# The output stage of a two-layer block in a written order of steps, with the group norm inside the gate's weights

## The chip, the cores and the metric

The kernel runs on one core of a Trainium2 chip. The metric is the time of one execution on the device in microseconds; the figure used is the median of several runs. A core has five engines that run side by side, each with its own queue of instructions worked off in order: TensorE (PE in the profile, its weight loads PEld), VectorE (DVE), ScalarE (ACT), GpSimd (POOL) and SyncE (SP), which here only issues DMAs. Engines wait for each other through semaphores.

## The reference

All data are float32. The input is a 256 x 256 image with 128 channels, that is 65,536 positions. Layer 0 is a triangle-like attention over group-normalized and layer-normalized pairs; layer 1 is a selective-scan block (four scan directions, 256 inner channels, 16 states). Both add to their input. The change concerns the end of layer 1, which is, per position:

```python
xz = gn(x1) @ w_in.T                 # group norm of layer 0's output x1, 32 groups over the whole image
xi, z = split(xz, 2)                 # 256 channels each
z = silu(z)                          # the gate
...                                  # xi goes through a convolution and four scans and becomes y
mu = y.mean(-1); var = ((y - mu) ** 2).mean(-1)
y = (y - mu) / sqrt(var + 1e-5) * ln_w + ln_b    # layer norm over 256 channels
out = x1 + (y * z) @ w_out.T         # 256 channels to 128
```

The group norm subtracts a mean and multiplies by an inverse deviation, one of each per channel once the statistics of the whole image are known (`gn2`, a tile of 128 x 2).

## The kernel before

The kernel goes through the image in stages, each of which keeps its result in device memory: group statistics, pair norm, attention, convolution, a transposition of scan inputs, the scans, and last `output`. The scans take nearly all of the time. They leave `mid_y`, the sum of the four directions, as 65,536 rows of 256 channels. `mid_x1T` is x1 with channels on the partitions (128 x 65,536).

`output` (L917 to L979) runs over 64 blocks of TB = 1024 positions, each with two chunks of T = 512. The loops are unrolled in the program, so every block has instructions of its own. The function is written block by block, one step after another; in which order the instructions of different blocks stand in each engine's queue is decided by a planner, which interleaves them by estimated costs. (In the scans the order is written out by hand, under `tc.manual_schedule()`; `output` has none.)

For one block:

- SyncE loads `xt` (0.5 MB, L938) and `y` (1 MB, eight tiles of 128 rows, L940). Both come from a pool with three buffers for each.
- VectorE makes `xn`, the group-normalized `xt` (L942), in one operation of 128 x 1024.
- For each of the eight row tiles of `y`, VectorE makes statistics (L946, L947). ScalarE takes the square root of the eight variances (Sqrt, L949), VectorE the reciprocal (L951), and then normalizes the eight row tiles in place (L953).
- For each chunk and each half h of the 256 channels: TensorE multiplies `wz` with `xn` into `pz` (L961), ScalarE makes Silu of it (L962). TensorE transposes four row tiles of `y` into `pt` (L965), ScalarE applies layer-norm scale and bias on the way out of PSUM into `yz` (Identity, L966).
- GpSimd multiplies `yz` by `z`, both halves in one operation (L969).
- TensorE multiplies with `wo`, the two halves added up in `pw` (L972). VectorE adds `xt` (`r`, L974), TensorE transposes it back (`pr`, L977), ScalarE copies it to `ot` (L978). After the second chunk ScalarE's queue issues the store to `out` (L979).

PSUM has two buffers each for `pz` and `pt`, one each for `pw` and `pr`. All SBUF tiles but the loads (`yz`, `z`, `r`, `ot`, `mv` and so on) have two buffers. Silu and Sqrt need different tables in ScalarE, and a table load is placed ahead of the first operation that needs the other one.

The start of `output` waits for the end of the scans: its buffers take the place of theirs, and `y` is read from what the last store of the scans wrote (L821).

Of the kernel before, what the change touches and what calls it, by code (L numbers as in the profile page):

```python
# [28 lines left out]
F32 = mybir.dt.float32  # L29
AF = mybir.ActivationFunctionType  # L30
ALU = mybir.AluOpType
AX = mybir.AxisListType
PSUM = bass.MemoryType.PSUM
ds = bass.ds

P = 128
N = 256
NT = N * N
C = 128
H, HD = 4, 32  # L40
DI = 256
NH = DI // P
# [4 lines left out]
T = 512  # L47
# [149 lines left out]
def attention(tc, io, c):  # L197


    nc = tc.nc  # L200
    NJ = N // P
    GB = 4
    RB = BLK // N
    with tc.tile_pool(name="c_w", bufs=1) as wp, tc.tile_pool(name="c_io", bufs=2) as iop, tc.tile_pool(
# [7 lines left out]
        for name in ("Wq", "Wk", "Wv", "Wg", "Wo"):  # L212
            w[name] = wp.tile([P, P], F32, name=name)
            nc.sync.dma_start(out=w[name], in_=io[name])
        bias = wp.tile([P, NJ, H, N], F32, name="bias")
        for jt in range(NJ):
            for h in range(H):
                nc.sync.dma_start(
                    out=bias[:, jt, h, :],
                    in_=io["bias"][h].rearrange("(t j k) -> t j k", t=NJ, k=N)[jt],  # L220
                )

        with tc.For_i(0, NB // GB, 1, name="rows") as it:
# [36 lines left out]
            def scores(g, s, r):  # L260
                qs, kt, _ = qkvs[g, s]
                sc = [ap.tile([P, H, N], F32, name="sc") for _ in range(NJ)]
                nm = [ap.tile([P, H], F32, name="nm") for _ in range(NJ)]
                for hh in range(H // 2):
# [650 lines left out]


def output(tc, io, c):  # L917
    nc = tc.nc
    out = io["out"].rearrange("b h w c -> (b h w) c")
    TB = 1024  # L920
    NJ = TB // P
    QJ = T // P
    with tc.tile_pool(name="f_w", bufs=1) as wp, tc.tile_pool(name="f_in", bufs=3) as inp, tc.tile_pool(
        name="f_sb", bufs=2
    ) as sb, tc.tile_pool(name="f_ps", bufs=2, space=PSUM) as psum, tc.tile_pool(
        name="f_po", bufs=1, space=PSUM
    ) as po:
        wz = wp.tile([P, DI], F32, name="wz")
        nc.sync.dma_start(out=wz, in_=io["w_inT"][:, DI : 2 * DI])
        wo = wp.tile([P, NH, C], F32, name="wo")  # L930
        nc.sync.dma_start(out=wo, in_=io["w_outT"].rearrange("(h p) c -> p h c", p=P))
        ln = wp.tile([P, 2, NH], F32, name="ln")
        nc.sync.dma_start(out=ln[:, 0, :], in_=io["ln_w"].rearrange("(h p) -> p h", p=P))
        nc.sync.dma_start(out=ln[:, 1, :], in_=io["ln_b"].rearrange("(h p) -> p h", p=P))
        for b in range(NT // TB):
            cols = slice(b * TB, (b + 1) * TB)
            xt = inp.tile([P, TB], F32, name="xt")
            nc.sync.dma_start(out=xt, in_=io["x1T"][:, cols])  # L938
            y = inp.tile([P, NJ, DI], F32, name="y")
            nc.sync.dma_start(out=y, in_=io["y"][cols, :].rearrange("(j p) c -> p j c", p=P))  # L940
            xn = sb.tile([P, TB], F32, name="xn")
            nc.vector.tensor_scalar(xn, xt, c.gn2[:, 0:1], c.gn2[:, 1:2], ALU.subtract, ALU.mult)  # L942
            st = sb.tile([P, NJ, 6], F32, name="st")
            mv = sb.tile([P, NJ, 2], F32, name="mv")
            for j in range(NJ):
                nc.vector.bn_stats(st[:, j, :], y[:, j, :])  # L946
                nc.vector.bn_aggr(mv[:, j, :], st[:, j, :])  # L947
            sd = sb.tile([P, NJ], F32, name="sd")
            nc.scalar.activation(sd, mv[:, :, 1], AF.Sqrt, bias=c.eps)  # L949
            rs = sb.tile([P, NJ], F32, name="rs")  # L950
            nc.vector.reciprocal(rs, sd)  # L951
            for j in range(NJ):
                nc.vector.tensor_scalar(y[:, j, :], y[:, j, :], mv[:, j, 0:1], rs[:, j : j + 1], ALU.subtract, ALU.mult)  # L953
            ot = sb.tile([P, NJ, C], F32, name="ot")
            for s in range(TB // T):
                cs = slice(s * T, (s + 1) * T)
                yz = sb.tile([P, NH, T], F32, name="yz")
                z = sb.tile([P, NH, T], F32, name="z")
                for h in range(NH):
                    pz = psum.tile([P, T], F32, name="pz")  # L960
                    nc.tensor.matmul(pz, wz[:, h * P : (h + 1) * P], xn[:, cs], start=True, stop=True)  # L961
                    nc.scalar.activation(z[:, h, :], pz, AF.Silu)  # L962
                    pt = psum.tile([P, QJ, P], F32, name="pt")
                    for j in range(QJ):
                        nc.tensor.transpose(pt[:, j, :], y[:, s * QJ + j, h * P : (h + 1) * P], c.ident)  # L965
                    nc.scalar.activation(  # L966
                        yz[:, h, :], pt.rearrange("p j t -> p (j t)"), AF.Identity, bias=ln[:, 1, h : h + 1], scale=ln[:, 0, h : h + 1]
                    )
                nc.gpsimd.tensor_tensor(yz, yz, z, ALU.mult)  # L969
                pw = po.tile([P, T], F32, name="pw")  # L970
                for h in range(NH):
                    nc.tensor.matmul(pw, wo[:, h, :], yz[:, h, :], start=(h == 0), stop=(h == NH - 1))  # L972
                r = sb.tile([P, T], F32, name="r")
                nc.vector.tensor_tensor(r, pw, xt[:, cs], ALU.add)  # L974
                pr = po.tile([P, QJ, C], F32, name="pr")
                for j in range(QJ):
                    nc.tensor.transpose(pr[:, j, :], r[:, j * P : (j + 1) * P], c.ident)  # L977
                nc.scalar.copy(ot[:, s * QJ : (s + 1) * QJ, :], pr)  # L978
            nc.scalar.dma_start(out=out[cols, :].rearrange("(j p) c -> p j c", p=P), in_=ot)  # L979


SCRATCH = {
# [14 lines left out]
@with_exitstack  # L997
def build(ctx: ExitStack, tc: tile.TileContext, io):
    const = ctx.enter_context(tc.tile_pool(name="const", bufs=1))
    c = load_consts(tc, const, io)  # L1000
    group_stats(tc, io, c)
    pair_norm(tc, io, c)
    attention(tc, io, c)
    conv(tc, io, c)
    swap(tc, io, "dc1", "dcT")
    scans(tc, io, c)
    output(tc, io, c)
# [45 lines left out]
```

## Time and profile before

| what | us |
|---|---|
| median of 3 runs | 29,773.57 |
| lowest and highest run | 29,766.73 and 29,790.43 |
| profiled execution | 29,807.18 |
| its span on the core | 29,805.5 |
| last store of the scans issued (L821) | 29,023.53 |
| first load of `output` issued (L929) | 29,027.80 |
| first and last `pw` product begin (L972) | 29,048.7 and 29,796.2 |

The span is the time from the first to the last instruction on the core. Times within it count from its start. Over the 760 us from 29,040 to 29,800 the engines are busy as follows:

| engine | busy us | share |
|---|---|---|
| TensorE | 649.8 | 85% |
| ScalarE | 569.8 | 75% |
| VectorE | 555.5 | 73% |
| GpSimd | 305.7 | 40% |
| DMA engines (mean of 16) | | 54%, 172 GB/s |

The granted clock of TensorE is 1.00 of full speed in this stretch (0.955 over the whole span). Matrix instructions are pipelined: one begins before the one ahead of it has ended, so their durations add up to more than the time they take. A line of the groups gives line, engine, operation, tiles written and read, shapes and count, then busy time and the mean of one, then the idle time of the engine just before them, and which instructions ended it. A line of the chain gives the start, the length and the instructions. A float32 product of 512 columns is two matrix instructions in the profile.

### The profile page before, as it was taken

The page shows a single profiled execution, that of the slowest core. Times are in us where ns is not written, and L with a number is a line of the kernel's source. Part 1 is how long each engine was busy: PE and PEld are TensorE (multiplying, and loading weights), DVE is VectorE, ACT ScalarE, POOL GpSimd, SP SyncE. Part 2 cuts the span into 40 slices and gives each one's busy share as a digit, 9 for nine tenths or more (in the row PEclk, how much of TensorE's full clock was granted, in tenths as well). Part 3 has the DMA queues.
Part 4 walks back from the last instruction along what each step waited for, and adds up shares of the span by engine and source line. Part 5 has one row for each costly group of instructions (what it writes and reads, how often), then busy time and mean ns, then how long its engine had stood idle before and what let it go on. Part 6 is the DMA issues. An engine that isn't in the chain of part 4 may idle for free. (4 is left out here: it accounts for less than half of the span.)

```text
span 29805.5 us, 535143 instructions
## 1 busy us (share of the span) xinstructions
PE 27420.7 (92%) x196490; PEld 22683.4 (76%) x196490; DVE 25716.6 (86%) x28349; ACT 25280.5 (85%) x49640; POOL 23015.2 (77%) x10118
## 2 busy tenths in 40 slices
PE   8888899699999999999999999999999999999998
PEld 3444444488888888888888888888888888888884
DVE  4555566599999999999999999999999999999997
ACT  5555422499999999999999999999999999999997
POOL 1333200299999999999999999999999999999984
PEclk8888899899999999999999999999999999999999
DMA  5000144433333333333333333333333333333335
GB/s 194 35 36 35 52 116 113 114 130 130 130 130 127 130 127 129 131 130 127 131 127 130 129 129 130 130 129 131 127 130 128 131 130 128 129 130 129 129 129 172
DMA packets 1924053, 3630.55 MB, mean 122 GB/s; under 512 B 532298, under 2 KB 1240010, under 8 KB 1889491
## 3 DMA queue, kind: packets, MB, share of 16 engines
q1 hardware_dynamic: 1424722, 3339.77, 32.9%
q10 hardware_dynamic: 496640, 255.88, 3.1%
q8 instruction: 1571, 25.74, 0.4%
q14 instruction: 1120, 9.17, 0.1%
HBM read 3002.42 MB, written 592.84 MB: 121 GB/s over the span
## 5 line engine op out<-in xcount | busy, mean ns | idle before, releaser
L784 POOL TENSOR_TENSOR hs<-hs,cc 128x1024 f32<-128x1024 f32 x8192 | 19303.7, 2374 | 1672.5 <-DVE state L783 1163.9
L781 DVE TENSOR_TENSOR_SCAN hs<-da,state,mm 128x1024 f32<-128x1024 f32 x8192 | 19227.4, 2347 | 1023.5 <-PE mm L771 694.9
L769 PE MATMUL mm<-dg,dxt 128*128 128x128 f32 x65536 | 9421.6, 288 | 1255.7 <-DVE hs L781 1019.1
L769 PEld LDWEIGHTS mm<-dg,dxt 128*128 128x128 f32 x65536 | 8249.9, 197 | 2747.3 <-DVE hs L781 2080.7
L762 ACT ACTIVATE da<-delta,A 128x1024 f32<-128x1024 f32 x8192 | 9342.2, 1140 | 91.2 <-PEq L903 59.8
L540 PE MATMUL y<-ident,hs 128*128 128x128 f32 x65536 | 8464.1, 274 | 0.0
L758 ACT ACTIVATE but<-dxt,bt 128x256 f32<-128x256 f32 x16384 | 8172.8, 499 | 11.4 <-DVE dxt L717 11.4
L540 PEld LDWEIGHTS y<-ident,hs 128*128 128x128 f32 x65536 | 7462.3, 142 | 0.2 <-POOL hs L784 0.2
L756 ACT ACTIVATE dg<-ident,bt 128x128 f32<-128x128 f32 x16384 | 6414.3, 391 | 0.2
L771 PE MATMUL mm<-ident,but 128*128 128x128 f32 x32768 | 5091.1, 279 | 0.0
L771 PEld LDWEIGHTS mm<-ident,but 128*128 128x128 f32 x32768 | 4006.1, 146 | 0.0
L306 POOL TENSOR_TENSOR an<-ex,rs 128x1024 f32<-128x1024 f32 x512 | 959.8, 1893 | 1989.2 <-DVE rs L304 1976.6
L673 PE MATMUL mm<-dt,dtw 9*128 9x512 f32 x4096 | 2032.7, 615 | 216.8 <-DMA bt<-mid_bk 185.6
L295 ACT ACTIVATE ex<-sc,nm 128x256 f32<-128x256 f32 x2048 | 1014.2, 497 | 781.5 <-DVE nm L280 779.1
L783 DVE COPY state<-hs 128x1 f32<-128x1 f32 x8192 | 1260.7, 154 | 280.6
L703 POOL TENSOR_TENSOR lw<-lw,e 128x1024 f32<-128x1024 f32 x512 | 1220.4, 2384 | 337.7 <-ACT lw L689 337.7
L673 PEld LDWEIGHTS mm<-dt,dtw 9*128 9x128 f32 x4096 | 680.7, 184 | 912.8 <-issue 725.0
L682 ACT ACTIVATE e<-mm 128x1024 f32<-128x1024 f32 x512 | 524.3, 1024 | 948.3 <-PE mm L673 940.3
L423 POOL MEMSET pad<- 128x10 f32 x32 | 3.7, 116 | 1647.7 <-PE ps L460 1637.0
L700 POOL TENSOR_TENSOR lw<-lw,w 128x1024 f32<-128x1024 f32 x512 | 1216.9, 2377 | 0.0
L460 PE MATMUL ps<-pad,w 128*128 128x512 f32 x2048 | 954.7, 610 | 162.1 <-ACT xi L448 162.1
L316 PEld LDWEIGHTS tp<-ident,an 128*128 128x128 f32 x4096 | 546.6, 159 | 525.9 <-issue 372.7
(135 smaller groups left out, 19146.7 us busy)
## 6 DMA issues: line engine op xcount, KB each, us to landing
cc<-mid_dc SPq DMA_DIRECT2D x2048, 512.0 KB
cc<-mid_dcT SPq DMA_DIRECT2D x2048, 512.0 KB
xk<-mid_xk SPq DMA_DIRECT2D x256, 1024.0 KB
yb<-mid_y SPq DMA_DIRECT2D x256, 1024.0 KB
mid_y<-yb SPq DMA_DIRECT2D x256, 1024.0 KB
xt<-mid_xT SPq DMA_DIRECT2D x64, 1024.0 KB
mid_xk<-xk ACTq DMA_DIRECT2D x32, 2048.0 KB
mid_y<-y ACTq DMA_DIRECT2D x32, 2048.0 KB
```

What stands on the lines that cost most here:

```text
L540: nc.tensor.matmul(out, in_, c.ident, is_transpose=True, start=start, stop=stop, skip_group_check=True)
L673: nc.tensor.matmul(pu[:, q : q + T], dtw[0 : DR + 1, k, h * P : (h + 1) * P], B.dt[0 : DR + 1, q : q + T], start=True, stop=True,)
L700: nc.gpsimd.tensor_tensor(B.lw[:, h, :], B.lw[:, h, :], B.w[:, h, :], ALU.add)
L703: nc.gpsimd.tensor_tensor(B.lw[:, h, :], B.lw[:, h, :], B.e[:, h, :], ALU.add)
L756: nc.scalar.activation(dg[:, j, :], c.ident, AF.Copy, scale=B.bt[:, B.slot(j), m : m + 1])
L758: nc.scalar.activation(bu[:, j, :], B.dxt[:, DJ + j, :], AF.Copy, scale=B.bt[:, at, m : m + 1])
L762: nc.scalar.activation(da, B.delta[:, h, :], AF.Exp, scale=A[:, B.S.k * NH + h, m : m + 1])
L769: nc.tensor.matmul(d1[:, j * P : (j + 1) * P], B.dxt[:, j, hc], dg[:, j, :], start=True, stop=True)
L771: nc.tensor.transpose(d1[:, j * P : (j + 1) * P], bu[:, j - DJ, hc], c.ident)
L781: nc.vector.tensor_tensor_scan(o, d0, d1, state[:, m, h : h + 1], ALU.mult, ALU.add)
L783: nc.vector.tensor_copy(state[:, m, h : h + 1], hs[:, h, last : last + 1])
L784: nc.gpsimd.tensor_tensor(hs[:, h, :], hs[:, h, :], ccs[m % 4], ALU.mult)
```

## The change

Only `output` is changed. It has these parts:

- **The group norm goes into the weights.** `wz` is multiplied once by the inverse deviation of each channel, and `bz`, minus the product of the scaled `wz` with the mean, becomes the bias of Silu. `xn` is no longer made: `pz` is the product of `wz` with `xt` itself.
- **The order is written by hand**, under `tc.manual_schedule()`: each engine gets its instructions in the order in which the program states them. A loop over steps u issues, for different chunks: the gate's product and the transposes of chunk u+1 (`gated`, one half before and one after the row products), the row products of chunk u+2 (`normalized`), `pw` and `r` of chunk u (`mixed`), `pr` and the copy of chunk u-1 (`stored`), and the statistics of chunk u+8 (`stats`). In each step with u % 4 = 1 the deviations of the next group of four chunks follow (`deviations`: one Sqrt and one reciprocal of 16 columns in the place of one of 8 for each block).
- **Statistics** are made as four `bn_stats` and then four `bn_aggr`, not in pairs.
- **Loads and stores.** `y` has seven buffers and is loaded six blocks ahead, `xt` has three and is loaded one block ahead, in the even steps. The store of `out` is issued by SyncE, in the same queue as the loads.

```diff
@@ def output(tc, io, c):
-    with tc.tile_pool(name="f_w", bufs=1) as wp, tc.tile_pool(name="f_in", bufs=3) as inp, tc.tile_pool(
-        name="f_sb", bufs=2
-    ) as sb, tc.tile_pool(name="f_ps", bufs=2, space=PSUM) as psum, tc.tile_pool(
+    with tc.tile_pool(name="f_w", bufs=1) as wp, tc.tile_pool(name="f_y", bufs=7) as yp, tc.tile_pool(
+        name="f_in", bufs=3
+    ) as inp, tc.tile_pool(name="f_sb", bufs=2) as sb, tc.tile_pool(name="f_pz", bufs=2, space=PSUM) as psum, tc.tile_pool(
         name="f_po", bufs=1, space=PSUM
     ) as po:
...
+        nc.vector.tensor_scalar(wz, wz, c.gn2[:, 1:2], None, ALU.mult)
+        bz = wp.tile([P, NH], F32, name="bz")
+        for h in range(NH):
+            off = po.tile([P, T], F32, name="pw")
+            nc.tensor.matmul(off[:, 0:1], wz[:, h * P : (h + 1) * P], c.gn2[:, 0:1], start=True, stop=True)
+            nc.vector.tensor_scalar(bz[:, h : h + 1], off[:, 0:1], -1.0, None, ALU.mult)
...
-            xn = sb.tile([P, TB], F32, name="xn")
-            nc.vector.tensor_scalar(xn, xt, c.gn2[:, 0:1], c.gn2[:, 1:2], ALU.subtract, ALU.mult)
...
+        def deviations(g):
+            rss[g] = sb.tile([P, QG * QJ], F32, name="rs")
+            nc.scalar.activation(rss[g], mvs[g][:, :, 1], AF.Sqrt, bias=c.eps)
+            nc.vector.reciprocal(rss[g], rss[g])
...
+        def gated(u, h):
...
+            nc.tensor.matmul(pz, wz[:, h * P : (h + 1) * P], columns(u), start=True, stop=True)
+            nc.scalar.activation(zs[u][:, h, :], pz, AF.Silu, bias=bz[:, h : h + 1])
...
+            if h == NH - 1:
+                nc.gpsimd.tensor_tensor(yzs[u], yzs[u], zs.pop(u), ALU.mult)
...
+        def stored(u):
...
+            if q == QB - 1:
+                nc.sync.dma_start(
+                    out=out[b * TB : (b + 1) * TB, :].rearrange("(j p) c -> p j c", p=P), in_=ots.pop(b)
+                )
+
+        with tc.manual_schedule():
+            NB2 = NT // TB
+            for b in range(2):
+                load_y(b)
+            load_x(0)
+            for u in range(-2 * QG, K + 2):
+                if u % QB == 0 and 0 <= u // QB + 6 < NB2:
+                    load_y(u // QB + 6)
+                if u % QB == 0 and 1 <= u // QB + 1 < NB2:
+                    load_x(u // QB + 1)
+                if 0 <= u + 1 < K:
+                    gated(u + 1, 0)
+                if 0 <= u + 2 < K:
+                    normalized(u + 2)
+                if 0 <= u + 1 < K:
+                    gated(u + 1, 1)
+                if 0 <= u < K:
+                    mixed(u)
+                if 0 <= u - 1 < K:
+                    stored(u - 1)
+                if 0 <= u + 2 * QG < K:
+                    stats(u + 2 * QG)
+                if u % QG == 1 and 0 <= u // QG + 1 < K // QG:
+                    deviations(u // QG + 1)
```

Here QG = 4, QB = 2 and K = 128 chunks. The rest of `gated`, `stats`, `normalized`, `mixed` and `stored` holds the operations of before, each for one chunk.

More of the change, by code (lines that the diff above doesn't have):

```diff
@@ L920, in output @@
     TB = 1024
-    NJ = TB // P
     QJ = T // P
-    with tc.tile_pool(name="f_w", bufs=1) as wp, tc.tile_pool(name="f_in", bufs=3) as inp, tc.tile_pool(
-        name="f_sb", bufs=2
-    ) as sb, tc.tile_pool(name="f_ps", bufs=2, space=PSUM) as psum, tc.tile_pool(
+    QB = TB // T
+    QG = 4
+    K = NT // T
+    with tc.tile_pool(name="f_w", bufs=1) as wp, tc.tile_pool(name="f_y", bufs=7) as yp, tc.tile_pool(
+        name="f_in", bufs=3
+    ) as inp, tc.tile_pool(name="f_sb", bufs=2) as sb, tc.tile_pool(name="f_pz", bufs=2, space=PSUM) as psum, tc.tile_pool(
         name="f_po", bufs=1, space=PSUM
@@ L934, in output @@
         nc.sync.dma_start(out=ln[:, 1, :], in_=io["ln_b"].rearrange("(h p) -> p h", p=P))
[L935 to L940, printed above, removed]
-            xn = sb.tile([P, TB], F32, name="xn")
[L942 to L979, printed above, removed]
@@ new lines, in output @@
+        nc.vector.tensor_scalar(wz, wz, c.gn2[:, 1:2], None, ALU.mult)
[4 more added lines that the diff above has]
+            nc.vector.tensor_scalar(bz[:, h : h + 1], off[:, 0:1], -1.0, None, ALU.mult)
+        xts, ys, mvs, rss, pts, zs, yzs, pws, rs_, prs, ots = {}, {}, {}, {}, {}, {}, {}, {}, {}, {}, {}
@@ new lines, in load_x, with load_y, rows, stats @@
+        def load_x(b):
+            xts[b] = inp.tile([P, TB], F32, name="xt")
+            nc.sync.dma_start(out=xts[b], in_=io["x1T"][:, b * TB : (b + 1) * TB])
+        def load_y(b):
+            ys[b] = yp.tile([P, TB // P, DI], F32, name="y")
+            nc.sync.dma_start(out=ys[b], in_=io["y"][b * TB : (b + 1) * TB, :].rearrange("(j p) c -> p j c", p=P))
+        def rows(u):
+            return ys[u // QB][:, u % QB * QJ : (u % QB + 1) * QJ, :]
+        def stats(u):
+            g, q = divmod(u, QG)
+            if q == 0:
+                mvs[g] = inp.tile([P, QG * QJ, 2], F32, name="mv")
+            y = rows(u)
+            st = sb.tile([P, QJ, 6], F32, name="st")
+            for j in range(QJ):
+                nc.vector.bn_stats(st[:, j, :], y[:, j, :])
+            for j in range(QJ):
+                nc.vector.bn_aggr(mvs[g][:, q * QJ + j, :], st[:, j, :])
@@ new lines, in deviations, with normalized @@
+        def deviations(g):
+            rss[g] = sb.tile([P, QG * QJ], F32, name="rs")
+            nc.scalar.activation(rss[g], mvs[g][:, :, 1], AF.Sqrt, bias=c.eps)
+            nc.vector.reciprocal(rss[g], rss[g])
+        def normalized(u):
+            g, q = divmod(u, QG)
+            y = rows(u)
+            for j in range(QJ):
+                x = q * QJ + j
+                nc.vector.tensor_scalar(
+                    y[:, j, :], y[:, j, :], mvs[g][:, x, 0:1], rss[g][:, x : x + 1], ALU.subtract, ALU.mult
+                )
@@ new lines, in columns @@
+        def columns(u):
+            return xts[u // QB][:, u % QB * T : (u % QB + 1) * T]
+        def gated(u, h):
+            if h == 0:
+                zs[u] = sb.tile([P, NH, T], F32, name="z")
+                yzs[u] = sb.tile([P, NH, T], F32, name="yz")
+            pz = psum.tile([P, T], F32, name="pz")
+            nc.tensor.matmul(pz, wz[:, h * P : (h + 1) * P], columns(u), start=True, stop=True)
+            nc.scalar.activation(zs[u][:, h, :], pz, AF.Silu, bias=bz[:, h : h + 1])
+            y = rows(u)
+            pt = psum.tile([P, QJ, P], F32, name="pt")
+            for j in range(QJ):
+                nc.tensor.transpose(pt[:, j, :], y[:, j, h * P : (h + 1) * P], c.ident)
+            nc.scalar.activation(
+                yzs[u][:, h, :],
+                pt.rearrange("p j t -> p (j t)"),
+                AF.Identity,
+                bias=ln[:, 1, h : h + 1],
+                scale=ln[:, 0, h : h + 1],
+            )
+            if h == NH - 1:
+                nc.gpsimd.tensor_tensor(yzs[u], yzs[u], zs.pop(u), ALU.mult)
@@ new lines, in mixed @@
+        def mixed(u):
+            pw = po.tile([P, T], F32, name="pw")
+            yz = yzs.pop(u)
+            for h in range(NH):
+                nc.tensor.matmul(pw, wo[:, h, :], yz[:, h, :], start=(h == 0), stop=(h == NH - 1))
+            rs_[u] = sb.tile([P, T], F32, name="r")
+            nc.vector.tensor_tensor(rs_[u], pw, columns(u), ALU.add)
+        def stored(u):
+            b, q = divmod(u, QB)
+            if q == 0:
+                ots[b] = sb.tile([P, TB // P, C], F32, name="ot")
+            pr = po.tile([P, QJ, C], F32, name="pr")
+            r = rs_.pop(u)
+            for j in range(QJ):
+                nc.tensor.transpose(pr[:, j, :], r[:, j * P : (j + 1) * P], c.ident)
+            nc.scalar.copy(ots[b][:, q * QJ : (q + 1) * QJ, :], pr)
+            if q == QB - 1:
+                nc.sync.dma_start(
+                    out=out[b * TB : (b + 1) * TB, :].rearrange("(j p) c -> p j c", p=P), in_=ots.pop(b)
+                )
```

## Prediction

> **What bounds the kernel now.** I read the page first: the span is 29,805.5 us, and its chain of waits (part 4) runs from the end back through `output` alone. So I cut the trace into stages. `output` begins when the last `mid_y` store has left (29,023.5 us) and its own first load is issued at 29,027.8; it ends with the span. It is some 778 us, 2.6% of the span: nothing in this change can be worth more. Within it I read the groups by shape, between 29,030 us and the end:
>
> ```profile
> L969 POOL TENSOR_TENSOR yz<-yz,z 128x1024 f32<-128x1024 f32 x128 | 305.7, 2399 | 470.0 <-ACT yz L966 248.7 <-issue 127.2 <-PE pz L961 63.6
> L961 PE MATMUL pz<-xn,wz 128*128 128x512 f32 x512 | 268.1, 607 | 27.4 <-ACT z L962 14.3 <-DVE xn L942 13.1
> L972 PE MATMUL pw<-yz,wo 128*128 128x512 f32 x512 | 250.0, 611 | 72.2 <-POOL yz L969 72.2
> L966 ACT ACTIVATE yz<-pt,ln 128x512 f32<-128x512 f32 x256 | 200.8, 786 | 44.6 <-PE pt L965 44.5
> L946 DVE BATCH_NORM_STATS2 st<-y 128x6 f32<-128x256 f32 x512 | 193.9, 403 | 127.8 <-DMA y<-mid_y 127.5
> ...
> L974 DVE TENSOR_TENSOR r<-pw,xt 128x512 f32<-128x512 f32 x128 | 87.5, 684 | 77.0 <-PE pw L972 76.9
> ...
> L962 ACT ACT_TABLE_LOAD x65 | 83.4, 1283 | 34.2 <-PE pz L961 33.1
> L949 ACT ACT_TABLE_LOAD x64 | 82.1, 1283 | 1.1
> ```
>
> Each engine has idle time that ends with another one: TensorE waits for the gate's product on GpSimd, GpSimd for ScalarE, VectorE for loads and for TensorE. No engine is full. The durations overlap within an engine, so the pace of work comes from the chain in order of time, here of one pair of chunks:
>
> ```profile
> 29411.51 1.98 PE pw L972 x4
> 29413.49 0.44 PE pt L965 x4
> 29413.93 0.86 PE pz L961 x2
> 29414.79 0.44 PE pr L977 x4
> 29415.23 1.72 PE pw L972 x4
> 29416.95 0.44 PE pt L965 x4
> 29417.38 0.86 PE pz L961 x2
> 29418.25 0.44 PE pr L977 x4
> ```
>
> The pieces abut: when nothing is missing, a logical product of 512 columns (two matrix instructions) costs 0.86 us and four transposes 0.44. A chunk of 512 positions has two `pz` (1.72), two `pw` (1.72), eight `pt` (0.88) and four `pr` (0.44): **4.76 us of TensorE**. The first `pw` starts at 29,048.7 us and the last of the 128 at 29,796.2, which is 747.5/127 = 5.89 us a chunk. So TensorE stands still 1.13 us per chunk, about 143 us in all, and that is the prize. It is lost because VectorE, ScalarE and GpSimd get a chunk's steps too late.
>
> **What is removed and moved.**
>
> *The group norm of x.* 64 `xn` products on VectorE go (0.73 to 0.81 us undisturbed, 1.24 mean). In their place stand one scaling of `wz`, two one-column products and two small `bz` operations before `y` arrives: about 2 us, under the first loads. Without that cover, 2 us once.
>
> *The work per chunk on the other engines.* VectorE: four pairs of statistics at 0.39 (the pitch of L946 and L947), four row products at 0.33 (eight took 2.67 at 29,042.9), `r` 0.60: 3.5 us. ScalarE: two Silu at 0.59, two Identity at 0.74, one copy 0.56, a quarter of the table loads and Sqrt 0.72: 3.9 us. GpSimd 2.35. All are under 4.76, and the written order gives each operand a lead: statistics eight chunks, row products two, the gate one, `pr` one chunk after `pw`. In a plain chunk the last `pt` ends 2.60 us into the step; seen 0.25 later and through the Identity (0.78) it starts GpSimd at 3.7, which ends 1.3 us into the next step, where `pw` is reached at 2.60 only. TensorE is then the bound.
>
> *Silu gets a bias.* No Silu with one is in the trace. From PSUM, Sigmoid without (L236) takes 597 ns, Ln and Square with one (L165, L159) 687. Bounds 0 and +0.18 us (the `yz` row, with bias and scale, has 786 against 603); I take the near rows, +0.09 each, or 0.18 a chunk.
>
> *Table loads.* 129 become 64 (Sqrt and Silu, once per four chunks). They still stand in ScalarE's path:
>
> ```profile
> 29422.50 0.60 ACT L962 ACTIVATE z<-pz 128x512 f32<-128x512 f32 x1 [0.21 <-POOL yz L969]
> 29423.12 1.28 ACT L949 ACT_TABLE_LOAD   x1
> 29424.41 0.30 ACT L949 ACTIVATE sd<-mv,eps 128x8 f32<-128x8 f32 x1
> 29425.04 0.78 ACT L966 ACTIVATE yz<-pt,ln 128x512 f32<-128x512 f32 x1 [0.33 <-PE pt L965]
> 29425.84 1.28 ACT L962 ACT_TABLE_LOAD   x1
> 29427.13 0.60 ACT L962 ACTIVATE z<-pz 128x512 f32<-128x512 f32 x1
> ```
>
> This is the place where the written order costs something. `deviations` comes at the end of a step, behind the copy of chunk c. Let TensorE start `pr` of c at 0. TensorE could reach `pw` of c+3 after 0.44 + gate of c+3 2.60 + `pw` 1.72 + `pr` 0.44 + gate of c+4 2.60 = 7.80 us. ScalarE: `pr` done and seen 0.69, copy 0.56, table 1.30, Sqrt 0.30, table 1.30, then both Silu and Identity of c+3 (0.59+0.72+0.59+0.78 = 2.68) = 6.83. GpSimd starts 0.1 later and takes 2.35, and 0.06 passes to TensorE: 9.34. **TensorE waits 1.54 us once per four chunks**, 31 times (the first deviations lie before the pipeline): 48 us.
>
> Here a rule of the Trainium skill speaks against the change. "ScalarE: Activation LUTs", section "What ACT_TABLE_LOAD costs", puts 1.38 us of draining on top of the 1283 ns. In the rows above the load starts 0.02 us after the previous operation's end, and the next starts at its end: a switch is 1.29. By the page the wait would be 1.54 + 2×1.38 = 4.3 us, 133 us in all, and nearly the whole prize would be gone. I take the row.
>
> *The order of the queues.* The store of `out` leaves ScalarE's queue (0.38 us an issue, 64 times, off its path) for SyncE's. There it waits for the copy, and behind it stand the `y` load six blocks ahead, which nobody misses, and the `xt` load of the block after next, which `pz` needs. The copy of an odd chunk ends 0.25+0.56 us after its `pr`, and `pz` of that `xt` comes two steps, 9.52 us, after `pr`: 8.7 us of room. Need: in the packet records an issue takes 1.1 us to its first packet, a store of 0.5 MB 1.85 us, and a `y` and `xt` pair on one queue 4.4 (both at the stage's start), 0.3 to be seen: 7.8. Hidden with 0.9 to spare, against nothing. On the high side I take 8.6 (2.1 MB at the 316 GB/s that 55% busy at 174 GB/s imply, plus 2 us).
>
> *The port between VectorE and GpSimd.* Eight row products took 2.67 us with GpSimd idle and, at 29,436.5, 4.03 with 1.6 us of a GpSimd product beside them. They exclude each other. In the written order a step's row products follow `r` and statistics and lie mostly between two GpSimd products; where they meet, at most 2.35 us is lost, and VectorE has 1.26 of slack a chunk, and a lead of a full step.
>
> *The start.* Four blocks of `y` and one of `xt` come before the first gate. With the first packet at 29,031.2, 2.9 us per `y` and 1.45 per `xt`, block 2 is in at 29,041.8; statistics of chunks 4 and 5 take until 29,045.1, the first row products until 29,046.6, the first gate until 29,048.2, ScalarE and GpSimd until 29,051.7: the first `pw` is **3.0 us later** than now.
>
> **The sum.** 29,051.7 + 127 × 4.76 (604.5) + 48 + the tail from the last `pw` to the end as now (9.3) = 29,713.5 against the span of 29,805.5: 92 us less. The profiled execution took 29,807.2 in all and the median of the runs is 29,773.57; I take the same 92 from the median: **29,681 us**.
>
> **The rivals.**
>
> 1. *As worked out* (0.58): 29,660 to 29,700.
>
> 2. *The table wait is hidden* (0.20), because later products let TensorE catch up. For it: ScalarE has some 0.8 us of slack a chunk. Against it: TensorE has none, being the bound. Then 29,713.5 - 48 = 29,665.5, or a median of 29,634.
>
> 3. *`xt` comes late* (0.10). For it: 0.9 us of room by the packets and almost none by the mean rate. If it lands 0.5 us late in each of 64 blocks, it costs up to 32 us: about 29,713; up to 29,740 with a full microsecond.
>
> 4. *No change* (0.07): draining as the page has it (29,766), or VectorE losing a whole GpSimd product per chunk, 3.5+2.35 = 5.85 us, today's pace. The rows with the loads abutting speak against the first; the second needs the row products to fall under GpSimd each time.
>
> 5. *Slower* (0.05): the single queue. If store, `y` and `xt` in a row only get the rate of the stage today, 174 GB/s, 2.1 MB take 12.1 us; with the 2 us to start and land and 0.8 from `pr` to copy, the loop of two steps closes in 14.9 instead of 11.8: 64 × 3.1, 29,972. It decides from 11.0 us from issue to landing. Against it: the start of the stage shows a lone queue at twice that rate.
>
> About 0.2% (60 us) is what a measurement can tell from no change. Rivals 1 and 2 and most of 3 are beyond it: faster 0.86, same 0.09, slower 0.05. The range runs from the hidden table wait, 29,632, to a late `xt`, 29,714.
>
> **What would show it.** The scans as before, `output` from 778 to about 686 us. TensorE at 93% busy in it, the `pw` pace at 5.14 us a chunk; its main idle time before `pw`, ended by GpSimd, some 31 times 1.5 us. 64 table loads at 1283 ns with no gap. Waits of `pz` for `xt` at zero. Wrong if `pz` waits for a DMA, if `pt` waits for row products, or if the gap around table loads is over 1.3 us.

## The result, and the profile after

| | before | after |
|---|---|---|
| median of 14 runs, us | 29,776.01 | 29,723.83 |
| lowest to highest | 29,766.73 to 29,808.80 | 29,694.35 to 29,763.23 |
| ratio, 95% interval | | 0.9981 (0.9973 to 0.9989) |
| span of the profiled execution | 29,805.5 | 29,711.9 |
| first load of `output` to the end of the span ("the stage") | 777.7 | 705.4 |
| first load to first `pw` | 20.9 | 26.8 |
| `pw` pace, us a chunk | 5.89 | 5.28 |
| last `pw` to the end | 9.3 | 8.6 |

The kernel is faster by 52 us, and the interval of the ratio lies clear of 1. The prediction was 29,681, a gain of 92, with a range that ended at 29,714: the direction was right, the measured time lies outside the range.

The groups by shape of the stage, from the same view: first one line of before, then the stage after.

```profile
L953 DVE TENSOR_SCALAR y<-y,mv,rs 128x256 f32<-128x256 f32 x512 | 193.8, 445 | 0.1
```

```profile
L980 DVE TENSOR_SCALAR y<-y,mv,rs 128x256 f32<-128x256 f32 x512 | 372.7, 788 | 1.2
...
L1012 PE MATMUL pw<-yz,wo 128*128 128x512 f32 x512 | 244.2, 599 | 26.4 <-POOL yz L1006 26.4
...
L997 PE MATMUL pt<-ident,y 128*128 128x128 f32 x1024 | 164.8, 277 | 22.9 <-DVE y L980 22.9
...
L972 ACT ACT_TABLE_LOAD x31 | 39.8, 1283 | 0.5
L993 ACT ACT_TABLE_LOAD x31 | 39.8, 1283 | 0.6
```

TensorE's wait for GpSimd before `pw` has shrunk from 72 to 26 us, and the table loads are halved. But the costliest group is now the 512 row products of the layer norm (VectorE). They were 445 ns each in the mean, and are 788 with the same shape and hardly any idle time ahead. The number of elements has not changed, so some of them stand still inside. TensorE now waits 22.9 us for them before `pt`, which the prediction had named as a sign of being wrong. The chain of waits of the stage goes through them. Here a stretch of it (start, length, instructions):

```profile
29306.91 0.60 DVE r L1014
29307.51 1.31 DVE st L966 x4
29308.82 0.28 DVE mv L968 x3
29309.10 3.33 DVE y L980 x4
29312.43 0.60 DVE r L1014
29313.03 1.31 DVE st L966 x4
29314.35 0.28 DVE mv L968 x4
29314.62 3.34 DVE y L980 x4
```

No TensorE in it: VectorE's steps abut. These two chunks take 5.5 us each, of which the four row products take 3.3 (0.33 each, or 1.3, when nothing is in the way). The mean step of the stage is shorter, 5.28. The timeline of the same moment shows what is in the way:

```profile
29309.02 3.41 DVE L980 TENSOR_SCALAR y<-y,mv,rs 128x256 f32<-128x256 f32 x4
...
29309.93 2.35 POOL L1006 TENSOR_TENSOR yz<-yz,z 128x1024 f32<-128x1024 f32 x1 [3.18 <-ACT yz L998]
```

GpSimd's product starts when three row products are through; the fourth takes some 2.4 us and ends just behind it. It happens in most steps: 111 of the 512 row products take over 1 us (16 before), in 82 of the 128 steps.

### The profile page after: what moved, and what is told of

Its sections match the earlier page's. It is cut to its first block, busy times and chain, and to the rows that moved or that the text cites. A ratio compares the mean times of both kernels' runs of the same rounds, so it can differ in the third digit from the quotient of the medians.

```text
span 29711.9 us, 535371 instructions
## 1 busy us (share of the span) xinstructions
PE 27375.6 (92%) x196494; PEld 22667.2 (76%) x196494; DVE 25806.2 (87%) x28256; ACT 25207.7 (85%) x49543; POOL 23018.2 (77%) x10118
```

## The experiments

All stage lengths are from the first load of `output` to the end of the span, in the profiled execution of that run; the pace is that of the copies (L978 before), first to last, over 127. (By `pw` the changed kernel has 5.28 and by the copies 5.25; only like is compared with like below.) Where a ratio is given, it was timed against the kernel before on the same chip.

| run | stage us | pace | ratio (95% interval) |
|---|---|---|---|
| kernel before | 777.7 | 5.88 | |
| before_again | 779.9 | 5.90 | 0.9998 (0.9989 to 1.0006) |
| changed kernel | 705.4 | 5.25 | 0.9981 (0.9973 to 0.9989) |
| after_again | 707.0 | 5.26 | 0.9977 (0.9968 to 0.9986) |
| no_rows | 693.7 | 5.14 | 0.9970 (0.9961 to 0.9979) |
| no_table | 659.9 | 4.89 | |
| no_both | 656.0 | 4.83 | |
| keep_xn | 783.5 | 5.86 | |
| fold_only | 861.5 | 6.56 | |
| early_dev | 663.6 | 4.92 | 0.9966 (0.9953 to 0.9979) |
| split | 690.0 | 5.13 | 0.9972 (0.9961 to 0.9983) |
| split_x2 | 642.0 | 4.75 | |
| split_x2_timed | 641.6 | 4.75 | 0.9952 (0.9938 to 0.9966) |
| best | 659.7 | 4.90 | 0.9961 (0.9948 to 0.9975) |

### How steady is the stage?

Both kernels again, unchanged.

> The kernel before, unchanged, to see how far its output stage (first load to end of span) and its scans vary from one profiled execution to the next. Theory A (the output stage is steady; what differs between executions is in the scans): stage 775 to 780 us as before (777.7), ratio 1.000 within 0.001. Theory B (the stage itself varies, and the profiled execution of before was a slow one in it): stage at 755 or less.

> The changed kernel, unchanged. Theory A: its output stage takes 700 to 712 us again (705.4), and the ratio comes nearer to 1 - 72/29776 = 0.9976 than to the 0.9981 measured first. Theory B (the stage is longer in executions that were not profiled): stage 715 to 730 us, ratio 0.998.

The stage repeats within 2.2 and 1.6 us: 777.7 and 779.9, 705.4 and 707.0. So the change takes **72 to 73 us** off it. What varies is what lies ahead: the first load of `output` comes at 29,027.8 and 29,021.9 us in the two profiles of the kernel before, at 29,006.5 and 29,036.2 in those of the changed one, with the same instructions up to there. Theory A holds for the stage. 72 us are a ratio of 0.9976, which both timings have in their intervals.

### Row products against GpSimd

```diff
                 if 0 <= u + 1 < K:
                     gated(u + 1, 0)
-                if 0 <= u + 2 < K:
-                    normalized(u + 2)
```

> Leaves out the row products (deviations from the mean times the inverse deviation); everything else stands, GpSimd's product and the table loads too. Port theory (VectorE is the bound, because its row products stand behind GpSimd's product, some 2 us a chunk): the pace falls from 5.30 to what the table wait leaves, 5.14 us a chunk, stage about 686 us, idle time of TensorE before pw ended by GpSimd some 31 times 1.5 us. Table theory alone (the row products cost nothing): no change, stage 705. If the table wait was over-estimated: pace near 4.76, stage 640.

The pace falls to 5.14, about the value that the prediction had for TensorE with the table wait alone. The idle time of TensorE in this run, from 29,070 to 29,650 us, in the list of who waited for whom (us in total, times, longest; two lines under 1 us are left out):

```profile
PE pw L1012 <- POOL yz L1006: 32.3, 27, 1.4
PE pz L992 <- DMA xt<-mid_x1T: 3.8, 6, 1.3
```

The wait for GpSimd comes once per four chunks. In the list it is 1.2 us in the mean; in the timeline of TensorE the step that has it is longer by more:

```profile
29303.76 1.88 PE L1012 MATMUL pw<-yz,wo 128*128 128x512 f32 x4
...
29310.04 1.98 PE L1012 MATMUL pw<-yz,wo 128*128 128x512 f32 x4 [1.36 <-POOL yz L1006]
```

These two starts are 6.28 us apart, plain ones 4.75; in the mean of the stage it is 1.52 more: the table wait, where and as long as it was worked out (1.54). The row products, which are at nothing in the sum, cost the changed kernel 11.7 us of its stage. By the pace of the copies it is 14 us (0.112 a chunk): without them the first copy comes 2.4 us later, in a longer start, part of it with TensorE at half speed.

### The table loads

```diff
-            nc.scalar.activation(rss[g], mvs[g][:, :, 1], AF.Sqrt, bias=c.eps)
+            nc.scalar.activation(rss[g], mvs[g][:, :, 1], AF.Identity, bias=c.eps)
```

`no_both` has this edit and that of no_rows.

> Leaves out the square root (Identity in its place[...]), so that ScalarE changes no table; all the rest as in the changed kernel. If the row products stand behind GpSimd by themselves in every step (the port keeps the two engines in that phase once it is reached): pace 5.2 to 5.3, stage 695 to 706 us. If it is the table wait that throws the steps out of phase and the port only then costs something: pace 4.76 to 4.85, stage 640 to 652 us. Without either effect of the port (the prediction's sum less 48): 638.

> Leaves out the square root and the row products. Port and table theory together: nothing but TensorE is left, pace 4.76 to 4.80, stage 640 to 648 us. If loads of xt are late at that pace (the rival of the prediction; the halved product showed them late up to 2.6 us behind a store whose copy the table loads delay): pz waits for the DMA, pace above 4.85.

no_table leaves out the square root itself. Without table loads the stage is 45.5 us shorter, and the row products are back at 0.41 us, though GpSimd's product is there as before. The groups of VectorE from 29,100 to 29,600 us, first of no_table, then of the changed kernel:

```profile
L980 DVE TENSOR_SCALAR y<-y,mv,rs 128x256 f32<-128x256 f32 x404 | 137.3, 404 | 0.9
L1014 DVE TENSOR_TENSOR r<-pw,xt 128x512 f32<-128x512 f32 x101 | 69.9, 692 | 134.0 <-PE pw L1012 134.0
```

```profile
L980 DVE TENSOR_SCALAR y<-y,mv,rs 128x256 f32<-128x256 f32 x378 | 282.3, 806 | 0.9
...
L1014 DVE TENSOR_TENSOR r<-pw,xt 128x512 f32<-128x512 f32 x95 | 64.6, 680 | 10.1 <-PE pw L1012 10.1
```

In no_table VectorE waits 1.3 us a chunk for `pw` (134.0 us over 101 `r`), and with that pause its row products stay clear of GpSimd: 5 of 512 take over 1 us. In the changed kernel the pause is gone and they meet. The two costs are not independent: by the pace of the copies, leaving out the row products is worth 14 us with table loads and 8 without (4.89 to 4.83; 3.9 by the stages, whose starts differ), and what is left without them is the `xt` load, for which TensorE waits 12 us in no_table and 4 in no_both, from 29,100 to 29,640. For the same reason the 45.5 us are not the table wait alone. The stand at the port is mainly what the table wait brings with it in this kernel; the last runs below show that it can come without one.

So at 4.83 to 4.89 a chunk there is still something above 4.76, and it is the `xt` load (16 waits of `pz` in no_table's list). The prediction's third rival is real as soon as the pace comes near TensorE's own.

### One half of the change at a time

keep_xn is the written order with `xn` still made (its operation goes into the even steps, ahead of the gate); fold_only is the planned order of before with the group norm in the weights:

```diff
...
-            xn = sb.tile([P, TB], F32, name="xn")
-            nc.vector.tensor_scalar(xn, xt, c.gn2[:, 0:1], c.gn2[:, 1:2], ALU.subtract, ALU.mult)
...
-                    nc.tensor.matmul(pz, wz[:, h * P : (h + 1) * P], xn[:, cs], start=True, stop=True)
-                    nc.scalar.activation(z[:, h, :], pz, AF.Silu)
+                    nc.tensor.matmul(pz, wz[:, h * P : (h + 1) * P], xt[:, cs], start=True, stop=True)
+                    nc.scalar.activation(z[:, h, :], pz, AF.Silu, bias=bz[:, h : h + 1])
...
```

> The changed kernel with xn still made on VectorE and not put into the weights. If VectorE with its stands at the port is the bound: 0.37 us a chunk more and perhaps one more stand per block, pace 5.65 to 6.2, stage 755 to 820 us, the gain gone. If TensorE and the table wait are the bound: pace 5.3, stage 706.

> The kernel before with the group norm put into the weights, order still planned. If the written order brings most of the gain: stage 755 to 778 us (before 778 to 780). If relief of VectorE by 0.37 us a chunk is what counts in either order: 0.37 x 128 = 47 us less, stage about 731.

Neither half gains anything alone (one profile of each). The written order with `xn` takes 783.5 us, 6 more than before. The pace is in the range of the first theory, but the way there is not the expected one alone: `xn` stands in VectorE's queue ahead of the row products, waits there for `xt` (29 us from 29,100 to 29,640), and `pz` waits for `xn` (44 us). VectorE is busy 88% of the time, so its load alone is not shown to be the bound. And TensorE's granted clock is 0.95: from 29,100 us to 12 us before the end there are 21 stretches of 3.4 us at half speed, each behind a standstill of 1.9 us or more. That is up to 36 us, nearly half of what keep_xn is behind the changed kernel. The fold alone takes **861.5 us, 84 more than before**, which neither theory had. The planner now places the instructions in another order, in which TensorE stands 1.6 us before `pw` once per block, and in most blocks its clock then falls. Two stretches of this run, the first 200 us long (us, busy time of PE, PEld, DVE, ACT, POOL with counts, granted clock, DMA share, GB/s):

```profile
29300.00:29500.00 200.00, 170.61 (x607) 89.07 (x606) 136.80 (x410) 139.52 (x198) 71.61 (x30) 0.91 0.52 161
...
29308.50:29311.90 3.40, 3.40 (x5) 1.24 (x4) 1.45 (x6) 0.64 (x1) 2.35 (x1) 0.50 0.00 0
```

and in its chain of waits:

```profile
29305.35 2.36 POOL yz L973
...
29307.76 3.10 PE pw L976 x4
29310.86 1.44 PE pz L965 x2
```

The four instructions of `pw` take 3.1 us here and 1.7 elsewhere. The busy 85% of TensorE hide that it works at half speed for a part of most blocks; only the clock (0.91, 1.00 in the kernel before) tells. There are 44 such stretches of 3.4 us, again up to 12 us before the end, 150 us in all: at half speed up to 75 us of work lost, nearly the whole 84. So what the fold would be worth at full clock in the planned order, this run doesn't show. Which of the planner's moves makes the standstill was not tried.

The other parts of the change (`y` six blocks ahead, the store in SyncE's queue, one pair of table loads for four chunks, the order of the statistics) were not tried one by one.

### Three ways out

*Deviations ahead of the copy.* ScalarE stands before the copy anyway (145 us in the stage, waiting for `pr`):

```diff
+                if u % QG == 1 and 0 <= u // QG + 1 < K // QG:
+                    deviations(u // QG + 1)
                 if 0 <= u - 1 < K:
                     stored(u - 1)
                 if 0 <= u + 2 * QG < K:
                     stats(u + 2 * QG)
-                if u % QG == 1 and 0 <= u // QG + 1 < K // QG:
-                    deviations(u // QG + 1)
```

> The changed kernel with the deviations one place earlier in their step, ahead of the copy in place of behind it; nothing left out. ScalarE then loads its tables in the time in which it waits for pr anyway: by the prediction's own durations pw of the third chunk is reached by GpSimd 7.96 us after pr begins, against 7.80 on TensorE, a wait of 0.16 in place of 1.54. Table theory: pace as without tables (4.89, where the xt load was the next wall) or a little less, stage 645 to 662 us, ratio about 0.996. Port theory alone (row products behind GpSimd whatever ScalarE does): pace 5.25, stage 705.

663.6 us, 42 less than the changed kernel, with nothing left out. The table wait is nearly hidden: `pw` waits for GpSimd no more in the list from 29,100 to 29,640 us. The row products are at 449 ns in the mean, near those of no_table, and `xt` is the next wall (12 waits of `pz`, 9.8 us).

*The product in halves.*

```diff
-            if h == NH - 1:
-                nc.gpsimd.tensor_tensor(yzs[u], yzs[u], zs.pop(u), ALU.mult)
+            nc.gpsimd.tensor_tensor(yzs[u][:, h, :], yzs[u][:, h, :], zs[u][:, h, :], ALU.mult)
```

> GpSimd's product in two halves, each as soon as its Identity is done. Port theory: the longest stand of a row product falls from about 2.3 to 1.2 us, VectorE needs 3.5 + 1.0 to 1.2 a chunk, under TensorE's 4.76, and the way from the table load to pw is 1.18 us shorter (wait 0.4 in place of 1.5): pace 4.85 to 5.0, stage 650 to 668 us. Table theory alone: 1.18 us less once per four chunks, stage 705 - 31 x 1.18 = 668 at most. If the total of GpSimd's time counts and not its piece: VectorE stands for as long as before, pace 5.3.

A miss: 690.0 us, 22 above the most that the table theory allowed. The waits of TensorE have moved to `pz`, for `xt`, and SyncE's queue shows why:

```profile
29302.92 0.38 SPq L1025 DMA_DIRECT2D out<-ot  x1
29303.41 0.52 SPq L954 DMA_DIRECT2D y<-mid_y  x1
29304.02 1.31 SPq L950 DMA_DIRECT2D xt<-mid_x1T  x1
29316.03 0.38 SPq L1025 DMA_DIRECT2D out<-ot  x1
29316.51 0.53 SPq L954 DMA_DIRECT2D y<-mid_y  x1
29317.13 1.31 SPq L950 DMA_DIRECT2D xt<-mid_x1T  x1
```

Two blocks' stores are 13.1 us apart, then 8.2 (the next one, at 29,324.3). `xt` is issued 1.1 us behind the store and lands 7.4 us later by the chain of waits, 8.5 from the store (9.8 for the block ahead of it). The prediction had 7.8 from the copy, and 8.6 on the high side. What it overlooked is that the copy of every second block's last chunk stands *behind the table loads and the gates that follow them* in ScalarE's queue, here until 29,315.4.

*And `xt` two blocks ahead*, with four buffers:

```diff
...
-                if u % QB == 0 and 1 <= u // QB + 1 < NB2:
-                    load_x(u // QB + 1)
+                if u % QB == 0 and 1 <= u // QB + 2 < NB2:
+                    load_x(u // QB + 2)
```

> The halved product, and xt loaded two blocks ahead with four buffers. If what held the halved product at 5.13 was the xt load behind a late store: no wait of pz for the DMA, pace 4.85 (4.76 and a table wait of about 0.4 per four chunks), stage 648 to 655 us. If it was not: 5.13, stage 690.

> The kernel of split_x2 again (product in halves, xt two blocks ahead, deviations where the change has them), now timed, since the one with all three parts ran slower (4.90 a chunk, VectorE without a pause). If its phase holds from one execution to the next: pace 4.75 to 4.80, stage 641 to 645 us, ratio 1 - 136/29790 = 0.9954. If VectorE can also fall into the slow phase here: pace 4.9 or more, stage 660.

Both executions: 642 us, TensorE's own pace, no wait of TensorE for another engine or a DMA from 29,100 to 29,640 us. It has the shortest stage of all, and is 0.48% below the kernel before; its interval (0.9938 to 0.9966) does not meet that of the changed kernel (0.9968 to 0.9986, on another set of runs).

*All three together.*

> All three: deviations ahead of the copy, product in halves, xt two blocks ahead. All theories together leave TensorE's 4.76 us a chunk: pace 4.76 to 4.82, stage 640 to 647 us, ratio 1 - 137/29776 = 0.9954. If VectorE at the port is a wall of its own: pace above 4.9.

A miss again: 659.7 us. Nothing waits for `xt` or a table, and it is slower than the same kernel without the earlier deviations. VectorE is busy without a pause, and its chain is once more statistics, row products and `r`:

```profile
29310.16 0.60 DVE r L1013
29310.76 1.31 DVE st L966 x4
29312.07 0.28 DVE mv L968 x4
29312.35 2.59 DVE y L980 x4
```

The row products take 768 ns each from 29,100 to 29,600 us, against 716 in split_x2, where VectorE is just as full but keeps TensorE's pace. So VectorE at the port is a wall of its own at 4.9 to 5.5 us a chunk, into which the steps can fall or not. What decides it between these two kernels is open; the timed intervals of the two overlap, the stages (two profiles of one, one of the other) do not.

## Why the prediction was wrong

**Point by point.** The direction, the place of the gain, and most terms of the sum stand:

- TensorE at 4.76 us a chunk when nothing is missing: split_x2 runs at it (4.75 by the copies).
- The table wait: 48 us by the sum. In no_rows its step is 1.52 us longer than a plain one, 47 us in 31 of them. (The 45.5 us of no_table and the 42 of early_dev are not this term alone: most stands at the port go with it, and waits for `xt` come in.) The row of the trace (1283 ns and no gap) was the right choice: in the timeline after, copy, load, Sqrt, load and Silu follow each other within 0.02 us,

```profile
29316.55 0.59 ACT L1024 COPY ot<-pr 128x512 f32<-128x512 f32 x1 [1.22 <-PE pr L1023]
29317.15 1.28 ACT L972 ACT_TABLE_LOAD   x1
29318.45 0.31 ACT L972 ACTIVATE rs<-mv,eps 128x16 f32<-128x16 f32 x1
29318.77 1.28 ACT L993 ACT_TABLE_LOAD   x1
29320.07 0.69 ACT L993 ACTIVATE z<-pz,bz 128x512 f32<-128x512 f32 x1
```

  so the draining that the page adds does not show here.
- Silu with a bias: +0.09 us by the near rows, 696 against 603 ns measured.
- `xt` in the changed kernel: hidden but for some 4 us, as taken. The need of 7.8 us was short, though: its items add up to 7.65, and 8.5 to 9.8 us were measured behind two stores in split, and the 2 us for start and landing on its high side are worked out from no row. (Rival 3's full microsecond would also come to 29,745, not 29,740.)

**The step that failed** is the one on *the port between VectorE and GpSimd*. It said that the row products "lie mostly between two GpSimd products" and that "at most 2.35 us is lost, and VectorE has 1.26 of slack a chunk, and a lead of a full step", and put nothing into the sum. The meeting itself was seen and its price known (a whole GpSimd product; the page "SBUF — State Buffer" of the Trainium skill, section "SBUF: two separate sides", says the same: the one that starts first keeps the shared ports for its whole instruction). What was wrong was the slack. The four row products, the statistics and `r` take 5.5 us in a step in which they meet (3.33 + 1.31 + 0.28 + 0.60), of which 2.0 are lost; against 4.76 that is 0.7 more than the slack holds, so one step out of phase is not made good in the next. The slack was laid out for a plain chunk only; the table wait, which the same text put at once per four chunks, delays a step, and with it row products of over 1 us come in 82 of 128 steps (in 5 without table loads, and in 5 with the loads moved). The `pw` pace came out at 5.28 in place of 5.14, 17.5 us in all. Leaving out the row products gives back 14 of them; another 4 are the waits for `xt`.

A smaller term was *the start*: the first `pw` comes 26.8 us after the first load, not 23.9. The first gates run at half speed, by the chain of waits and the granted clock (the 0.50 and 1.00) after:

```profile
29027.09 1.71 PE pz L992 x2
29028.80 0.85 PE pt L997 x4
...
29032.18 0.86 PE pz L992 x2
29033.04 0.44 PE pt L997 x4
```

```profile
29025.00:29032.00 7.00, 6.35 (x16) 3.65 (x17) 6.96 (x27) 2.84 (x4) 1.40 (x1) 0.50 1.09 348
29032.00:29040.00 8.00, 8.00 (x32) 4.18 (x32) 5.88 (x18) 4.83 (x8) 4.21 (x3) 1.00 0.82 282
```

TensorE has been mostly idle since the scans. The page "TensorE: Matmul & The Clock Gate" (Part 1) of the Trainium skill has it that the clock is held back until TensorE has been busy for about 3.4 us; here it takes longer, until 29,032.0, 6.4 us behind the first `pt` at 29,025.7. At half speed that is an estimated 3.2 us lost. The sum used the rows of the stage at full clock. With 0.7 us less at the end these make 17.5 + 2.9 - 0.7 = 19.7, the difference between the 705.4 us measured and the 685.7 predicted for the stage.

**The other 20 us**, between the 72 of the stage and the 52 measured, are not seen in the stage. Its first load comes between 29,002 and 29,045 us in the fourteen profiles here, behind the same scans; the three runs with the planned order have a mean of 29,024 and the eleven with the written order one of 29,025. The two timings of the changed kernel gave 0.9981 and 0.9977, and 72 us lie in both intervals. So this part is scatter as far as the record shows. The prediction's range counted unknown costs only and left the scatter out, though the three runs shown and the profiled execution (29,767 to 29,807) already spread over 40 us. It decided which side of the range's end the time fell on: 72 us off the median of those three runs is 29,701.6, inside the range. Had it fallen there, the port would still have been missing from the sum.

**The rivals.** The hidden table wait (0.20) did not come by itself, but early_dev shows that it takes one move. The late `xt` (0.10) is not in the changed kernel and is the next wall behind it. "VectorE losing a whole GpSimd product per chunk" was put under *No change* with 5.85 us; it came true in 82 of 128 steps, and the mean ended at 5.28. The slower single queue did not come.

## What to carry to other kernels

Count the time that an engine stands at a shared port into its budget per step, and compare it with the slack for a step that something else has just delayed, not only for a plain one: a small periodic stall (here a table load, once in four chunks) can keep two engines colliding in between. When a hand-written order removes one bound, look at what follows a blocked instruction in each queue, DMA queues too: a store that waits for a late copy makes the load behind it late. And two edits can be worth nothing or less alone and a gain together, so a part that fails by itself is not yet refuted: look first at what else it moved, as here the granted clock.

## What was not expected of the hardware

- A short standstill of TensorE can cost clock. Between 29,100 us and 12 us before the end, the runs whose longest standstill is under 1.6 us (the kernel before, up to 1.56, and the changed one, 1.37, among them) have no stretch at half speed. fold_only has 58 standstills of 1.6 to 1.9 us and 44 stretches of 3.4 us at half speed, keep_xn 27 of 1.9 to 2.2 us and 21 stretches. In split nine, of 1.7 to 2.6 us, are followed by only two. So length alone does not decide it; what else does was not tried.
- VectorE's row product (256 columns of float32) takes 0.33 us when it is free, the statistics of the same row 0.33 too. Only the row product stands still beside GpSimd; four statistics take 1.31 us whether GpSimd is at work or not.
